# Two engines' queues in written order: TensorE and SyncE in the attention loop of a one-core decoder

## The chip, the cores and the metric

The kernel runs on one core of a Trainium2 chip. A core has TensorE (PE: matrix products, with PEld for the loading of its weights), VectorE (DVE), ScalarE (ACT), GpSimd (POOL) and SyncE (SP, which here only issues DMA transfers). Each engine works through its own list of instructions and waits on semaphores for the others. PSUM is the memory that TensorE writes and VectorE and ScalarE read; it has eight banks. The metric is the device time of the whole program in microseconds (us), as the median of the runs.

## The reference: what is computed

One decoder layer on x of 16 sequences x 128 positions x 256 channels, in float32:

- `x = layernorm(x + attn(x))`, where attn is a gated delta rule with 16 key heads and 32 value heads of 128 channels;
- `x = layernorm(x + xattn(x, ctx))`, a cross attention;
- `x = layernorm(x + ffn(x))`, a mixture of seven experts (two for each token) and one shared expert.

The change touches the first part alone. There the input is projected to q, k and v (`x @ w_qkv`), convolved over four positions in each channel, and put through SiLU; `beta = sigmoid(x @ w_b)` and the decay `g = -exp(A_log) * softplus(x @ w_a + dt_bias)` come from two small projections. The recurrence over positions is

```
S = S * exp(g_t)
delta = (v_t - k_t S) * beta_t
S = S + k_t^T delta
o_t = q_t S
```

and the output is `o * silu(x @ w_z)`, normalised by its root mean square, times `norm_w`, times `w_out`.

## The kernel before

**Units and slots.** The sequences form four groups of four (`G`, `NG`). A unit is one group and one key head with its two value heads, so there are 64 units (`NU`). The recurrence isn't run position by position: for each unit, products of keys and queries with their decays (`pk`, then `lp`) give a lower triangular system, whose diagonal blocks of 32 x 32 are inverted for four units at a time (class `Group`: `begin` transposes the blocks (`Tp`) and forms the factors `bp`, `nbp`; `step` runs on GpSimd, and for the first group of four half of it on VectorE; `turn` transposes the result to `Tt`). The solve itself goes in four block rows: `pt` (multiply by the inverse blocks, `solve`) and `pu` (subtract what earlier rows give, `substitute`).

**The pipeline.** The attention is one loop over slots, `for s in range(NU + DELAY + 3)` (line 548), 74 turns. In slot s the loop works on different units at different stages: on `a` = unit s (projection of k and q, `pjkq`; scan of the decays, `decay`; products), on `v` = s - 6 (projection and convolution of v, `pjv`, `yv`, `vT`), on `m` = s - 7 (transposed values `pv`, first block row), on `p` = s - 8 (middle block rows; gate, `pjz`, `zs`), on `q` = s - 9 (last block row, `attend`: `po`, `og`, their squares `sqs`), and on `o` = s - 10 (`rms_end`, `output`: `pp`, added into `acc`). `psq` sums squares for the unit behind and for `o`. In the written order TensorE's list of a slot is: psq, pjkq of k, pjkq of q, pt (first), pp0 and pp1, po0, pjv0, pjz0, pu (second), pjv1, pp2 and pp3, pt (second), po1, pjz1, pk, pv0, then the next slot's pu (first) and pv1.

**Buffers in PSUM.** Five banks, tag `ps`, go round among pt, pu, pp, po, pk and pv; two banks, tag `pj`, among the projections; one, tag `sm`, holds psq. A projection's bank is free once its readers have finished: for k and q an eviction on ScalarE and three taps (`scalar_tensor_tensor`, line 356) on VectorE, for v two evictions on ScalarE and two taps on VectorE, for z one activation on ScalarE.

**Loads.** SyncE issues each unit's weights (`load_kq`, `load_v`, `load_z`, `load_o`) and decays (`load_dec`), two buffers each. The decays come by way of DRAM: `gates` (line 172) computes beta and the decays of a group, and stores the latter to `dec_d`; `gates([0])` stands ahead of the loop, `gates([1, 2, 3])` in slot 4. The rows of `w_out` are scaled by `norm_w` (`scale_wo`, line 160: two loads to `wor`, one activation on ScalarE, two stores to `wo_d`), in written order in slots 5 to 12; `load_o` reads `wo_d`. `load_x` brings the other groups' part of x in slots 1 to 3.

**What sets the order.** The program is recorded in the order in which Python writes it, and a scheduler then orders each engine's list by priorities and by a model of costs, within what data and buffers permit. `tc.manual_schedule(engines={Pool})` (line 547) excludes GpSimd in the attention loop: its list keeps the written order. TensorE, VectorE, ScalarE and SyncE are ordered by the scheduler. In the program that results, TensorE's list in most slots differs little from the written one: pp2 stands ahead of pjv1 everywhere; in one slot of four the second pu and pp2 stand ahead of pjv0 and pjz0; in another ahead of pjz0 alone; there the second pt is cut into pieces with pp3, po1 and pjv1 between. On SyncE the loads of `scale_wo` for the first two pieces, the three `load_x` and first loads of v and z stand at the head of the loop's list.

Of the kernel before, what the change touches and what calls it, by code (L numbers as in the profile page):

```python
# [18 lines left out]
HK, HV = 16, 32  # L19
G = 4  # L20
# [4 lines left out]
U = 4  # L25
NB, BS = 4, 32
DELAY = 7
# [9 lines left out]
def bc(ap, shape):  # L37
    return ap.to_broadcast(shape)
# [3 lines left out]
def decoder_kernel(  # L42
# [7 lines left out]
    nc = tc.nc  # L50
# [34 lines left out]
    def load_x(g):  # L85
        nc.sync.dma_start(out=acc[:, g * G : (g + 1) * G, :], in_=xv[:, g * G : (g + 1) * G, :])
# [28 lines left out]
    with ExitStack() as st:  # L115
# [6 lines left out]
        def bank(shape, name):  # L122
            return ps.tile(shape, F32, tag="ps", name=name)
# [4 lines left out]
        def transposed_x(g):  # L128
            xT = att.tile([P, 2, 512], F32, tag="xT", bufs=2, name=f"xT{g}")
            for kc in range(2):  # L130
                pt = bank([P, G, P], f"pxT{kc}_{g}_{len(xTs)}")
                for b in range(G):
                    pe.transpose(pt[:, b, :], acc[:, g * G + b, kc * P : (kc + 1) * P], ident)
                dst = xT[:, kc, :].rearrange("p (b t) -> p b t", b=G)
                if kc == 0:
                    act.copy(dst, pt)
                else:
                    vec.tensor_copy(dst, pt)
            return xT

        dec_d = dram.tile([HV, B, S], F32, name="dec_d")
# [30 lines left out]
        def gates(gs):  # L172

            n, b0 = len(gs), gs[0] * G

            def flat(tag, i):
                t = sb.tile([P, G, P], F32, tag=tag, bufs=3, name=f"gt{tag}{i}_{b0}")
                return t.rearrange("p b t -> p (b t)")[:, : n * P]

            apre, tabs, decT = flat("u0", 0), flat("u1", 1), flat("u1", 2)  # L180
            a3 = apre.rearrange("p (b h) -> p b h", h=HV)
            t3 = tabs.rearrange("p (b h) -> p b h", h=HV)
            for i, g in enumerate(gs):
                xT = transposed_x(g)
                if g == 0:
                    xTs[0] = xT
                pab = bank([P, G, 64], f"pab{g}")
                for b in range(G):
                    for kc in range(2):
                        pe.matmul(pab[:, b, :], lhsT=xT[:, kc, b * P : (b + 1) * P],  # L190
                                  rhs=wba[:, kc, :], start=(kc == 0), stop=(kc == 1))
                act.activation(beta[:, g * G : (g + 1) * G, :], pab[:, :, 0:32], AF.Sigmoid)
                vec.tensor_tensor(a3[:, i * G : (i + 1) * G, :], pab[:, :, 32:64],
                                  bc(dtb[:, None, :], [P, G, HV]), ALU.add)
            act.activation(tabs, apre, AF.Abs)
            act.activation(tabs, tabs, AF.Exp, scale=-1.0)
            act.activation(tabs, tabs, AF.Ln, bias=1.0)
            vec.scalar_tensor_tensor(out=tabs, in0=apre, scalar=0.0, in1=tabs,
                                     op0=ALU.max, op1=ALU.add)
            vec.tensor_tensor(t3, t3, bc(expa[:, None, :], [P, n * G, HV]), ALU.mult)  # L200
            act.activation(tabs, tabs, AF.Exp)
            pdt = bank([P, n, P], f"pdt{b0}")
            for i in range(n):
                pe.transpose(pdt[:, i, :], tabs[:, i * P : (i + 1) * P], ident)
            d3 = decT.rearrange("p (g t) -> p g t", t=P)
            vec.tensor_copy(d3, pdt)
            vec.memset(d3[:, :, 0:1], 0.0)
            for b in range(G):
                nc.sync.dma_start(
                    out=dec_d[:, b0 : b0 + n * G, :].rearrange("h (g b) t -> b h g t", b=G)[b],  # L210
                    in_=d3[b * HV : (b + 1) * HV, :, :])

        def behind(inst, after):

# [317 lines left out]
        def at(n):  # L532
            return units[n] if 0 <= n < NU else None
# [3 lines left out]
        for k in range(4):  # L537
            pe.transpose(pcw[:, k, :], cwr[:, :, k], ident[:64, :64])
        vec.tensor_copy(cw.rearrange("p c k -> p k c"), pcw)
        gates([0])  # L540
        units[0].load_dec()
        PIECES = 5
        sqs = None
        done = None


        with tc.manual_schedule(engines={mybir.EngineType.Pool}):
            for s in range(NU + DELAY + 3):
                a, v, m = at(s), at(s - DELAY + 1), at(s - DELAY)
                p, q, o = at(s - DELAY - 1), at(s - DELAY - 2), at(s - DELAY - 3)  # L550
# [7 lines left out]
                def piece(i):  # L558
                    if inv is None:
                        return  # L560
                    at_ = ph * PIECES + i
                    if at_ == 0:
                        inv.begin()
                    if k == 0:

                        if at_ == 0:
                            inv.negate(vec)
                            for j in range(1, 31):
                                last = inv.step(j, vec if j <= 15 else pool)
                                if j == 15:  # L570
                                    a.after = last
                            inv.norms()
                            inv.end()
                        return
                    if at_ == 1:
                        inv.negate(pool)
                    n = 3 * PIECES - 3
                    if 1 <= at_ <= n:
                        for j in range(1 + 30 * (at_ - 1) // n, 1 + 30 * at_ // n):
                            inv.step(j, pool)  # L580
                    if at_ == 2 * PIECES - 1:
                        inv.norms()
                    if at_ == n:
                        inv.end()

                if at(s + 1) is not None:
                    at(s + 1).load_kq()
                    at(s + 1).load_dec()
                if 0 < s < NG:
                    load_x(s)  # L590
                if s == U:
                    piece(0)
                    gates([1, 2, 3])
                if a is not None:
                    if U < s <= U + HK // 2:
                        scale_wo(s - U - 1)
                    if a.hk == 0 and a.g > 0:
                        xTs[a.g] = transposed_x(a.g)
                if v is not None:
                    v.load_v()  # L600
                if p is not None:
                    p.load_z()
                if q is not None:
                    q.load_o()
                jobs = [(m, 0, 0), (p, 1, 1), (p, 0, 2), (q, 1, 3)]
                substitute(f"pu{s}_0", jobs[1:])
                if m is not None:
# [67 lines left out]
    def bank2(shape, name):  # L675
# [4 lines left out]
                      in_=ctx_512.rearrange("b s d -> s b d"))  # L680
# [14 lines left out]
    for i, src in enumerate((bup, bgate)):  # L695
        nc.sync.dma_start(out=brw[:, i].rearrange("p e n -> p (e n)"),
                          in_=src.rearrange("e n -> (e n)").partition_broadcast(P))
# [27 lines left out]
    for t in xg:  # L725
        for i in range(0, TILES, 4):
            n = min(4, TILES - i)
            nc.sync.dma_start(out=t[i * P : (i + n) * P, :].rearrange("(t p) d -> p t d", p=P),
                              in_=zero[:, :n, :])
# [310 lines left out]
    for n in range(-LEAD, len(steps) + 3):  # L1040
# [18 lines left out]
        if n - 3 >= 0 and n % 2 == 1:  # L1059
            m = (n - 3) // 2  # L1060
# [238 lines left out]
```

## Time and profile before

| | us |
|---|---|
| median of the runs | 2191.08 |
| the runs | 2190.01, 2191.08, 2192.49 |
| profiled execution, its own time | 2189.38 |
| profiled execution, span | 2186.8 |
| TensorE busy over the span | 2040.9 |
| slots 10 to 63 (222.24 to 1572.10) | 1349.86 |
| slots 64 to 73, to 1750 | 177.9 |

Times in a profile count from the start of the span; what lies around the span (2.6 us here) is in the execution's own time. A row of the timeline gives start, length, engine, line, operation, output and inputs, how many instructions are folded into it, and in brackets for how long the engine had been idle and what released it. A row of the stages gives a stretch, its length and each engine's busy time in it, and at its end the TensorE clock granted (1.00 is full speed), the share of the DMA engines and GB/s. The chain of waits follows the last instruction back to what released it, step by step, and says which engine each piece of the span falls to.

The profile divides into four: a ramp to 222 us in which the first units pass through the pipeline, the first inversion is awaited, and TensorE is often idle; the steady stage; the drain, in which the last units leave the pipeline; and from 1750 us on the cross attention and the experts.

### The profile page before, as it was taken

The page shows a single profiled execution, that of the slowest core. Times are in us where ns is not written, and L with a number is a line of the kernel's source. Part 1 is how long each engine was busy: PE and PEld are TensorE (multiplying, and loading weights), DVE is VectorE, ACT ScalarE, POOL GpSimd, SP SyncE. Part 2 cuts the span into 40 slices and gives each one's busy share as a digit, 9 for nine tenths or more (in the row PEclk, how much of TensorE's full clock was granted, in tenths as well). Part 3 has the DMA queues.
Part 4 walks back from the last instruction along what each step waited for, and adds up shares of the span by engine and source line. Part 5 has one row for each costly group of instructions (what it writes and reads, how often), then busy time and mean ns, then how long its engine had stood idle before and what let it go on. Part 6 is the DMA issues. An engine that isn't in the chain of part 4 may idle for free.

```text
span 2186.8 us, 40366 instructions
## 1 busy us (share of the span) xinstructions
PE 2040.9 (93%) x14688; PEld 1242.5 (57%) x14688; DVE 1740.3 (80%) x3223; ACT 1316.1 (60%) x2696; POOL 1077.0 (49%) x1639
## 2 busy tenths in 40 slices
PE   4559999999999999999999999999989879989997
PEld 2324556566565666665666656656656534448873
DVE  4657889898999989898999989898856667866545
ACT  4536666667666667666676666676656445554431
POOL 0136473838465564739384655648372143352222
PEclk7779999999999999999999999999999979999998
DMA  6412222222222222222221222222011070013321
GB/s 195 137 48 54 59 59 71 61 65 66 59 64 68 64 64 64 62 69 59 68 64 59 71 61 68 64 59 59 30 40 30 23 262 1 1 56 105 110 80 58
DMA packets 140660, 150.72 MB, mean 69 GB/s; under 512 B 14184, under 2 KB 111472, under 8 KB 140464
## 3 DMA queue, kind: packets, MB, share of 16 engines
q1 hardware_dynamic: 133456, 135.37, 21.9%
q0 software_dynamic: 3072, 8.39, 1.2%
q10 hardware_dynamic: 3936, 4.38, 0.6%
q8 instruction: 118, 1.93, 0.4%
q14 instruction: 78, 0.64, 0.1%
HBM read 125.82 MB, written 22.28 MB: 68 GB/s over the span
## 4 chain that ended last, share of the span: by engine, by line
PE 72%; POOL 10%; DVE 8%; ACT 4%; issue 3%; DMA 3%; SPq 0%; ACTq 0%; POOLq 0%; DVEq 0%
PE pp L467 9%; PE pjv L339 8%; PE pjz L339 8%; PE pjkq L339 8%; PE pt L520 6%; PE po L452 5%; PE pu L505 5%; PE pk L399 4%; PE psc L787 3%; POOL Tp L277 2%; POOL tmp L275 2%; PE pv L439 2%; PE psq L482 2%; PE prg L1123 2%; PE pru L1123 2%
## 5 line engine op out<-in xcount | busy, mean ns | idle before, releaser
L524 ACT COPY u<-pt 32x512 f32<-32x512 f32 x512 | 294.4, 575 | 57.1 <-PE pt L520 48.4
L339 PE MATMUL pjkq<-xT,wkq 128*128 128x512 f32 x512 | 246.0, 621 | 55.9 <-issue 47.3
L509 DVE TENSOR_TENSOR u<-u,pu 32x512 f32<-32x512 f32 x384 | 263.6, 687 | 37.9 <-PE pu L505 27.0
L365 POOL TENSOR_TENSOR yv<-yv,y2v 128x508 f32<-128x508 f32 x128 | 161.8, 1264 | 255.2 <-DVE yv L356 231.8
L467 PE MATMUL pp<-wo,og 128*128 128x256 f32 x1024 | 272.1, 395 | 0.0
L277 POOL TENSOR_TENSOR Tp<-Tp,tmp 128x240 f32<-128x240 f32 (+14 forms) x465 | 253.6, 545 | 36.4
L275 POOL TENSOR_TENSOR tmp<-Tp 128x240 f32<-128x240 f32 (+14 forms) x465 | 239.6, 515 | 62.0 <-DVE Tp L277 33.8
L356 DVE SCALAR_TENSOR_TENSOR ykq<-pjkq,cw,ykq 128x504 f32<-128x504 f32 (+2 forms) x384 | 266.2, 725 | 2.8 <-ACT ykq L349 2.3
L356 DVE SCALAR_TENSOR_TENSOR yv<-pjv,cw,yv 128x504 f32<-128x504 f32 (+1 forms) x256 | 188.9, 738 | 98.7 <-ACT y2v L353 91.6
L339 PE MATMUL pjv<-xT,wv 128*128 128x512 f32 x512 | 250.2, 612 | 16.8 <-issue 7.0
L471 DVE SCALAR_TENSOR_TENSOR acc<-pp,rstd,acc 128x256 f32<-128x256 f32 x512 | 231.5, 477 | 42.9 <-POOL rstd L459 37.1
L459 POOL TENSOR_TENSOR rstd<-var,m_half 128x8 f32<-128x8 f32 x64 | 105.4, 1648 | 320.7 <-DVE ss L493 272.3
L339 PE MATMUL pjz<-xT,wz 128*128 128x512 f32 x512 | 243.7, 598 | 5.9 <-issue 5.9
L366 ACT ACTIVATE vT<-yv 128x512 f32<-128x512 f32 x128 | 80.7, 630 | 252.2 <-POOL yv L365 252.2
L467 PEld LDWEIGHTS pp<-wo,og 128*128 128x128 f32 x1024 | 183.5, 190 | 78.5 <-issue 57.2
L339 PEld LDWEIGHTS pjkq<-xT,wkq 128*128 128x128 f32 x512 | 93.1, 194 | 184.1 <-issue 173.9
L402 DVE TENSOR_TENSOR lp<-pk,e 128x512 f32<-128x512 f32 x256 | 159.3, 682 | 39.7 <-PE pk L399 38.6
L520 PE MATMUL pt<-u,Tt 32*32 32x128 f32 x4096 | 176.2, 272 | 1.6 <-ACT u L442 1.0
L520 PEld LDWEIGHTS pt<-u,Tt 32*32 32x32 f32 x4096 | 116.4, 104 | 105.5 <-issue 35.1
L384 DVE TENSOR_TENSOR_SCAN e<-dec,ident 128x512 f32<-128x512 f32 x128 | 158.4, 1278 | 8.2 <-DMA dec<-dec_d 6.5
L452 PE MATMUL po<-lp,u 128*128 128x128 f32 x1024 | 152.2, 285 | 0.0
L442 ACT ACTIVATE u<-pv,nk 128x128 f32<-128x128 f32 x512 | 147.3, 374 | 6.5 <-PE pv L439 5.8
(226 smaller groups left out, 3619.6 us busy)
## 6 DMA issues: line engine op xcount, KB each, us to landing
dec<-dec_d SPq DMA_DIRECT2D x64, 512.0 KB, 5.2
wkq<-in_L_attn_w_qkv_dram SPq DMA_DIRECT2D x128, 128.0 KB, 5.1
wv<-in_L_attn_w_qkv_dram SPq DMA_DIRECT2D x64, 256.0 KB, 2.6
wz<-in_L_attn_w_z_dram SPq DMA_DIRECT2D x64, 256.0 KB, 2.6
wo<-wo_d SPq DMA_DIRECT2D x64, 256.0 KB, 2.7
rx<-xg SPq DMA_DIRECT2D x44, 128.0 KB, 2.1
yg<-ry SPq DMA_DIRECT2D x44, 128.0 KB, 1.7
xg<-zero SPq DMA_DIRECT2D x10, 512.0 KB, 7.8
```

What stands on the lines that cost most here:

```text
L275: eng.tensor_tensor(tv, bc(T[:, j + 1 :, j : j + 1], [P, n, j]), bc(T[:, j : j + 1, 0:j], [P, n, j]), ALU.mult)
L277: return eng.tensor_tensor(T[:, j + 1 :, 0:j], T[:, j + 1 :, 0:j], tv, ALU.add)
L339: pe.matmul(pj.rearrange("p b t -> p (b t)"), lhsT=ws[kc], rhs=xTs[self.g][:, kc, :], start=(kc == 0), stop=(kc == 1))
L356: inst = vec.scalar_tensor_tensor(out=y[:, :, d:], in0=pj[:, :, : P - d], scalar=c[:, k : k + 1], in1=y[:, :, d:], op0=ALU.mult, op1=ALU.add)
L365: pool.tensor_tensor(y[:, :, 1:], y[:, :, 1:], y2[:, :, 1:], ALU.add)
L402: self.made = vec.tensor_tensor(self.lp[:, r, hf * 2 : hf * 2 + 2], pk, bc(self.e[r][:, hf * 2 : hf * 2 + 2, None, :], [P, 2, 2, P]), ALU. ...
L452: pe.matmul(po[:, b, :], lhsT=self.u_[r][:, b, :], rhs=self.lp[:, r, b, 1, :], start=True, stop=True)
L467: pe.matmul(pp[:, r, :], lhsT=self.og[:, r, b, :], rhs=self.wo[:, r, :], start=True, stop=True)
L471: vec.scalar_tensor_tensor(out=a, in0=pp[:, r, :], scalar=self.rstd[:, r, b : b + 1], in1=a, op0=ALU.mult, op1=ALU.add)
L509: vec.tensor_tensor(u.u_[r][blk], u.u_[r][blk], pu[blk], ALU.subtract)
L520: pe.matmul(pt[blk, b, :], lhsT=groups[u.n // U].Tt[blk, 8 * u.u + G * r + b, :], rhs=u.u_[r][blk, b, :], start=True, stop=True)
L524: act.copy(u.u_[r][blk], pt[blk])
```

## The change

- In the attention loop TensorE and SyncE keep the written order, as GpSimd does. VectorE and ScalarE are still ordered by the scheduler.
- The loads of v, z and w_out of a slot are written one slot earlier: behind the next unit's `load_kq` and `load_dec` come `load_v` for unit s - 5, `load_z` for m and `load_o` for p.
- `gates` returns the function that stores the decays. Group 0's are stored at once; those of groups 1 to 3, computed in slot 4, are stored in slot 5 (`U + 1`), behind the loads just named.

```diff
-            for b in range(G):
-                nc.sync.dma_start(
-                    out=dec_d[:, b0 : b0 + n * G, :].rearrange("h (g b) t -> b h g t", b=G)[b],
-                    in_=d3[b * HV : (b + 1) * HV, :, :])
+
+            def store():
+                for b in range(G):
+                    nc.sync.dma_start(
+                        out=dec_d[:, b0 : b0 + n * G, :].rearrange("h (g b) t -> b h g t", b=G)[b],
+                        in_=d3[b * HV : (b + 1) * HV, :, :])
+
+            return store
...
-        gates([0])
+        gates([0])()
         units[0].load_dec()
         PIECES = 5
         sqs = None
+        stores = []
...
-        with tc.manual_schedule(engines={mybir.EngineType.Pool}):
+        with tc.manual_schedule(engines={mybir.EngineType.Pool, mybir.EngineType.PE,
+                                         mybir.EngineType.SP}):
...
                 if at(s + 1) is not None:
                     at(s + 1).load_kq()
                     at(s + 1).load_dec()
+                if at(s - DELAY + 2) is not None:
+                    at(s - DELAY + 2).load_v()
+                if m is not None:
+                    m.load_z()
+                if p is not None:
+                    p.load_o()
+                if s == U + 1:
+                    for store in stores:
+                        store()
                 if 0 < s < NG:
                     load_x(s)
                 if s == U:
                     piece(0)
-                    gates([1, 2, 3])
+                    stores.append(gates([1, 2, 3]))
...
-                if v is not None:
-                    v.load_v()
-                if p is not None:
-                    p.load_z()
-                if q is not None:
-                    q.load_o()
```

## The prediction

> **What bounds the kernel now.** I read the page first (chain of waits, busy shares), then busy time by stage, then the timelines of SyncE, ScalarE, VectorE and TensorE in the stages that the change touches. The page:
>
> ```profile
> PE 2040.9 (93%) x14688; PEld 1242.5 (57%) x14688; DVE 1740.3 (80%) x3223; ACT 1316.1 (60%) x2696; POOL 1077.0 (49%) x1639
> PE 72%; POOL 10%; DVE 8%; ACT 4%; issue 3%; DMA 3%; SPq 0%; ACTq 0%; POOLq 0%; DVEq 0%
> ```
>
> TensorE (PE) is the bound over all, but by stage the picture differs (columns: stretch, its length, busy time of PE, its weight loads, DVE, ACT, POOL, then PE's clock and DMA):
>
> ```profile
> 28.00:74.00 46.00, 21.71 (x77) 11.27 (x76) 30.23 (x48) 20.04 (x34) 2.74 (x9) 0.76 0.65 178
> 155.00:222.24 67.24, 59.48 (x410) 31.99 (x410) 52.69 (x80) 44.44 (x95) 38.05 (x60) 0.95 0.22 56
> 222.24:1572.10 1349.86, 1336.11 (x10391) 816.89 (x10390) 1217.88 (x2048) 924.29 (x1895) 794.36 (x1180) 1.00 0.23 63
> 1572.10:1750.00 177.90, 163.66 (x1401) 101.88 (x1400) 109.33 (x207) 92.18 (x188) 71.65 (x90) 0.98 0.10 30
> ```
>
> The ramp (slots 0 to 9, to 222 us) is bound by latencies; in the steady stage (slots 10 to 63) PE is busy 99%; in the drain it waits again. From 1743.5 us, the last attention matmul, PE's and ACT's lists are the same in both programs: nothing is counted there.
>
> **The ramp.** The timelines of before's SyncE and ScalarE (start, length):
>
> ```profile
> 9.24 1.02 SPq L166 DMA_DIRECT2D wor<-in_L_attn_w_out_dram  x2
> 25.83 0.88 SPq L166 DMA_DIRECT2D wor<-in_L_attn_w_out_dram  x2
> 28.29 1.74 SPq L209 DMA_DIRECT2D dec_d<-gtu  x4
> 31.25 0.88 SPq L316 DMA_DIRECT2D dec<-dec_d  x2
> ...
> 16.38 1.15 ACT L168 ACTIVATE wor<-wor,normw 128x1024 f32<-128x1024 f32 x1 [6.68 <-DMA wor<-in_L_attn_w_out_dram]
> ```
>
> The scheduler had put the first w_out scalings ahead of everything: ACT idles 6.68 us for them before the gates' sigmoid, and the decays are stored at 28.29 only. In written order they stand in slots 5 to 12. Following ACT's five table loads and activations from where pab is ready, the store goes out at about 23.4 (−4.8; bounds 0 and −6.7, the whole wait) and the first scan at 31.7 instead of 37.8. The three other x loads, which stood ahead of wkq1, now follow a unit's decays; the groups 1 to 3 are wanted in slot 4, past 75 us, so that is free. Their decays' stores move to slot 5, behind wv0: first read in slot 16, hidden by ten slots; if that cover were gone, a late load costs its landing, 5.2 us.
>
> Against this, PE can no longer run a later unit's projections ahead. One ramp slot in strict order: psq 0.43, two projections 4 x 1.02 = 4.1, the second's eviction and three taps 0.69 + 3 x 0.74 = 2.9, SiLU 0.63, pk 3.78, wait for the squares about 0.6: 12.4 us, at half clock. Before, lp1, lp2, lp3 end at 47.1, 62.1 and 76.4; I get 48 (the scans and products of unit 0 end at about 35.5, and a slot follows), 60.9 and 73.5, with some 0.3 of hand-overs in each. So the first inversion (Tp0) starts at 75.5 instead of 80.2; DVE's and POOL's steps are the same, and POOL ends at 119.3 instead of 123.3. Group 1's transposition (Tp1, 179.15) is now followed at once by its small ones: nbp1 comes 4 us after it, not 6, at about 176.5 instead of 185; POOL's inversion paces pv1 of slot 9, 36.5 us later: 213 against 221.7, −8.5. Eight scalings of 1.15 us each now lie in slots 5 to 12: 9.2 us of ACT work, of which I take a third as on the path (ACT is 66% busy there): +3 (bounds 0 and 9.2). **Ramp: −5.5** (bounds −14, if the whole 6.7 of the wait and an 8 us earlier inversion carry through and no scaling costs; and +4, if the scalings cost 9 and the earlier nbp1 gives 5).
>
> The clock in that stage: after 12 us of idle PE runs at half, and with some 4 us of idle it is mixed:
>
> ```profile
> 44.00:56.00 12.00, 0.00 (x0) 0.00 (x0) 8.82 (x14) 4.94 (x10) 1.83 (x6) 0.50 0.73 212
> ...
> 56.21 2.04 PE L339 MATMUL pjkq<-xT,wkq 128*128 128x512 f32 x2 [17.22 <-issue]
> 68.91 1.67 PE L339 MATMUL pjkq<-xT,wkq 128*128 128x512 f32 x2 [4.10 <-issue]
> ```
>
> The Trainium skill ("TensorE: Matmul & The Clock Gate", "HAM oscillation — how this bites in real kernels") says that idle gaps beyond some 3.4 us drop the clock, over and over. It speaks against this change, whose in-order PE idles 4 to 5 us in each ramp slot; the second row agrees only in part (1.67 us, between 1.0 and 2.04). By the rule all three ramp slots stay slow, as I took them; by that row their 4.1 + 3.8 us of matmuls would take 0.82 of it, 1.4 less each, and the sum be lower by 4.
>
> **The steady stage.** Before's list is already near the written one. Four slots, from psq to psq, repeat: 24.06, 24.37, 24.92, 26.25 = 99.6 us. The rows of one undisturbed slot add up to 24.0 (psq .78, pjkq 3.64, two pt 2.0, pp 3.66, two po 2.0, pjv 3.59, pjz 3.53, two pu 2.0, pk 1.72, pv 1.12). So the cycle holds 3.6 us above 4 x 24.0 = 96.0, and **the change breaks even if the in-order waits of four slots sum to 3.6**. Those 3.6 are the price of going around DVE. In the fourth slot:
>
> ```profile
> 879.70 1.05 PE L452 MATMUL po<-lp,u 128*128 128x128 f32 x8
> 881.33 1.96 PE L339 MATMUL pjv<-xT,wv 128*128 128x512 f32 x4 [0.57 <-issue]
> 883.21 1.07 PE L505 MATMUL pu<-u,lp 128*32 128x128 f32 x24
> 884.21 1.13 PE L467 MATMUL pp<-wo,og 128*128 128x256 f32 x4
> 885.18 1.88 PE L339 MATMUL pjz<-xT,wz 128*128 128x512 f32 x4
> 887.86 0.40 PE L520 MATMUL pt<-u,Tt 32*32 32x128 f32 x2
> ...
> 878.64 1.97 DVE L246 STREAM_TRANSPOSE Tp<-ldg 128x1024 f32<-128x1024 f32 x1
> 883.42 0.73 DVE L356 SCALAR_TENSOR_TENSOR ykq<-pjkq,cw,ykq 128x500 f32<-128x500 f32 x1
> ```
>
> The inversion's transposition (1.97 us) delays the convolution taps that free the two pj banks; PE ran pu and pp2 meanwhile, and cut pt (a pair cut off takes 0.33 of PE's time, inside the block 0.06). In written order pjv0 and pjz0 stand ahead of pu: pjv0 waits 0.6 as now, pjz0 waits for the tap that ends at 884.15, 1.1 behind pjv0's end: 24.0 + 1.7 + 0.1 = 25.8 (−0.46). In the third slot the transposition Tt (2 us) makes DVE late in the same way; PE, which found pu and pp2 to do, now waits 1.3 for ykq0 before pjv0: 25.5 (+0.6). In the first and second slot written order has pjv1 directly behind pu, and pp2 behind it; pjv1 takes the bank of pjz0, which ACT's zs0 frees (0.60, plus the hand-over, behind pjz0's end), and pu covers 1.0 of it. ACT reaches zs0 late by its squares: a wait of 0.54 in the first (+0.45 net of a cut less), 0.35 in the second (−0.05 net). Behind each of these waits stand pp, pt and po, so DVE's og and subtractions start later too; they have 10% of slack. Sum +0.55 a cycle, 13.5 cycles: **+7** (bounds: −1 a cycle, where the waits are half of what I count, −13; +1.6, where each of the waits costs a quarter of a microsecond more to wake from, +21). I take a value near the middle, since three of the four waits are read from the ends of rows that stand where they stood.
>
> The loads: SyncE's wo load waits in slot s for pp3 (bank of two), and the next slot's kq, dec, v and z loads stand behind it. Each is issued a slot (24 us) before use and lands in 2.6 to 5.2 us: nothing, as long as that distance stays; if it is gone, about 5 us a slot.
>
> The Trainium skill (same page, "Step-by-step: what each phase is for") says that matmuls stay in program order and only weight loads are pulled ahead. By it none of these waits can be filled by the chip, 4.2 us a cycle; the 0.57 us above, with pu ready behind it, agrees.
>
> **The drain.** In slot 66 DVE's written neighbours change: Tt15, which waits for POOL, now stands ahead of pp1's last accumulation and of og, not behind.
>
> ```profile
> 1626.92 0.68 DVE L454 TENSOR_TENSOR og<-po,zs 128x512 f32<-128x512 f32 x1
> 1631.22 1.93 DVE L287 STREAM_TRANSPOSE Tt<-Tp 128x1024 f32<-128x1024 f32 x1 [3.61 <-POOL Tp L283]
> ```
>
> og then comes at 1633, not 1627, and with it ACT's squares, zs0 and pjv1 behind those; of the 6 us about 5 stay, less 0.1 in each of the five other slots: **+4.5** (bounds −2, where POOL is done earlier, and +8).
>
> **Sum.** −5.5 + 7 + 4.5 = +6. The profiled execution lasted 2189.4 (span 2186.8), 1.7 below the median of 2191.1: 2195.4 by the profile, 2197 as a median.
>
> **The rivals.** (1) Faster: the in-order waits are shorter than the work-arounds. DVE orders its taps anew once pu comes later; with waits of 2.4 instead of 4.2 a cycle, 1.2 under break-even, steady gives −16; ramp −8, drain +4: −20, 2171 (2165 to 2186). For it: PE's own cuts are the visible loss of the fourth slot; against: the taps that pjz0 waits for end where the scan, Tp and pjkq put them, and none of these moves. (2) Same: before's list was near the written one (6098 rows of PE against 5998 after), ramp and steady cancel: 2187 to 2195. (3) Much slower: DVE, 90% busy in the steady stage, is pushed by each PE wait and pushes back; 0.35 a slot more, 54 slots, +19 on +6: 2216 and above. For it: 1217.88 of 1349.86; against: DVE still idles 2.5 us a slot ahead of yv. It decides from some 2.4 us of DVE delay a slot on.
>
> **How the numbers follow.** 0.2% (4.4 us) is about what can be told from no change. The forecast 45% (own range 2195 to 2207), faster 30%, same 15%, much slower 10%. Faster is 0.30, same 0.15, slower 0.55. The range runs from 2174, leaving out the lower third of the first rival, to 2215, leaving out most of the third.
>
> **What would show it.** In the profile after: the first decay store at about 23 and Tp0 near 75 us; psq of slot 10 near 217; slots of about 25.8, 24.6, 24.3 and 25.5, with waits of pjz0 and pjv0 for ykq and of pjv1 for zs; pt whole (x32); in slot 66 og behind Tt. Wrong if pjv0, pjz0 and pjv1 start without waits, or if SyncE's loads show up as what PE waits for.

## The result, and the profile after

The changed kernel takes 2239.9 us (median; 2238.6 to 2240.5) against 2190.6 for the kernel before: a ratio of 1.022, 95% interval 1.021 to 1.023. It is 49 us slower. The prediction was 2197, with a range of 2174 to 2215; the sign was the likelier one, the size was not in the range. The profiled execution has a span of 2238.5, 51.7 more than before; where those lie can be counted from the start of one slot's psq on TensorE to that of the next:

| stage | before | after | difference | predicted |
|---|---|---|---|---|
| to psq of slot 11 | 248.3 | 253.4 | +5.1 | −5.5 |
| slots 11 to 63 | 1323.8 | 1364.1 | +40.3 | +7 |
| slot 64 to the last psq | 168.9 | 173.9 | +5.0 | +4.5 |
| from there to the end | 445.8 | 447.1 | +1.3 | 0 |

The page of the changed kernel, busy shares and chain of waits:

```profile
PE 2025.4 (90%) x14688; PEld 1243.3 (56%) x14688; DVE 1740.7 (78%) x3223; ACT 1324.3 (59%) x2696; POOL 1080.1 (48%) x1639
PE 57%; POOL 18%; DVE 11%; ACT 7%; issue 5%; DMA 2%; ACTq 0%; SPq 0%; POOLq 0%; DVEq 0%
```

TensorE does the same instructions in 15.5 us less busy time (2040.9 to 2025.4), and yet its share of the chain falls from 72% to 57%; POOL, DVE, ACT and "issue" take the rest. TensorE's waits in the steady stage, after (total, number, longest, in us):

```profile
PE pjv L343 <- issue: 26.2, 27, 1.5
PE pjv L343 <- ACT zs L435: 16.4, 41, 0.5
PE pjz L343 <- issue: 14.3, 23, 1.0
PE pt L524 <- DVE u L513: 5.3, 6, 1.4
PE pt L524 <- DVE lp L406: 5.2, 3, 1.7
PE pjv L343 <- ACT u L528: 0.6, 1, 0.6
```

and before:

```profile
PE pjv L339 <- issue: 7.0, 13, 0.6
PE pjz L339 <- issue: 5.9, 14, 2.0
```

That is 68.0 us of waits against 12.9, +55.1. Busy time in the same stage (slots 10 to 63, 1349.9 us before and 1389.1 after) falls from 1336.1 to 1320.9, −15.2. The stage's loss (39.2) is the one less the other, but for waits too small for the list. The trade that the prediction weighed is best read off one cycle of four ordinary slots (length, then TensorE's busy time; before, then after):

```profile
799.10:898.70 99.60, 98.78 (x770) 60.35 (x769) 89.62 (x150) 68.34 (x142) 59.04 (x89) 1.00 0.24 64
819.37:920.43 101.06, 96.78 (x770) 59.46 (x769) 89.26 (x150) 68.88 (x142) 59.63 (x89) 1.00 0.22 63
```

The cuts and re-orderings had cost 2.0 us of busy time a cycle, some 26 in 13 cycles; the waits rise from 0.8 to 4.3 a cycle. In the sum of the stage only 15 of the 26 are seen, since TensorE's busy time in three long slots (below) is some 11 us higher than in others.

**An ordinary slot.** TensorE in a slot of the fourth kind (`s % 4` of 0), changed kernel:

```profile
490.09 1.05 PE L456 MATMUL po<-lp,u 128*128 128x128 f32 x8
491.73 1.95 PE L343 MATMUL pjv<-xT,wv 128*128 128x512 f32 x4 [0.58 <-issue]
494.65 1.95 PE L343 MATMUL pjz<-xT,wz 128*128 128x512 f32 x4 [0.97 <-issue]
496.53 1.07 PE L509 MATMUL pu<-u,lp 128*32 128x128 f32 x24
...
490.92 0.71 DVE L360 SCALAR_TENSOR_TENSOR ykq<-pjkq,cw,ykq 128x500 f32<-128x500 f32 x1
493.81 0.74 DVE L360 SCALAR_TENSOR_TENSOR ykq<-pjkq,cw,ykq 128x500 f32<-128x500 f32 x1
```

The profile names no releaser for these two waits ("issue"), but the ends do: the third tap of k ends at 491.63 and pjv0 starts at 491.73, the third of q at 494.55 and pjz0 at 494.65. pjv0 and pjz0 wait 0.58 and 0.97 us for the taps that free their banks, with pu behind them; the prediction had 0.6 and 1.1. Four slots (`s % 4` of 1, 2, 3 and 0) now take 24.5, 25.0, 25.7 and 25.9 = 101.1 us, against 99.6 before and a forecast of 24.6, 24.3, 25.5 and 25.8 = 100.2.

**Three slots that are not ordinary.** Slots 26, 42 and 58 take 31.6, 31.9 and 32.4 us; before, they took 25.3 each. They alone are 20 of the 51.7 us. Slot 26 on VectorE and TensorE:

```profile
638.66 0.59 DVE L111 TENSOR_SCALAR acc<-acc,mva,rsa 128x256 f32<-128x256 f32 x1 [6.31 <-POOL rsa L106]
639.17 2.47 DVE L406 TENSOR_TENSOR lp<-pk,e 128x512 f32<-128x512 f32 x4
...
640.59 0.37 PE L524 MATMUL pt<-u,Tt 32*32 32x128 f32 x2 [1.73 <-DVE lp L406]
642.41 3.35 PE L524 MATMUL pt<-u,Tt 32*32 32x128 f32 x30 [1.44 <-DVE u L513]
645.69 3.22 PE L471 MATMUL pp<-wo,og 128*128 128x256 f32 x8
...
643.12 0.17 PEld L524 LDWEIGHTS pt<-u,Tt 32*32 32x32 f32 x2 [0.54 <-DVE u L513]
643.85 1.46 PEld L524 LDWEIGHTS pt<-u,Tt 32*32 32x32 f32 x26 [0.55 <-DVE u L513]
```

and before, at the end of the same slot instead of its start:

```profile
644.01 2.04 DVE L111 TENSOR_SCALAR acc<-acc,mva,rsa 128x256 f32<-128x256 f32 x4
```

L111 is the layernorm of the group that has just been finished (unit 15, 31 or 47): four multiplications, which need a power that GpSimd computes (rsa). The scheduler, which still orders VectorE, put the first of them ahead of a unit's products lp. VectorE stands for 6.31 us, and with it the products, the subtractions of pu behind them and TensorE. Then pt and pp, which take 1.08 and 1.99 us in other slots, take 3.35 and 3.22. The stages around them (length, busy times, then TensorE's clock) and the two rows of weight loads (PEld) tell why:

```profile
638.60:642.41 3.81, 0.63 (x4) 0.14 (x3) 3.69 (x7) 0.73 (x2) 2.96 (x7) 0.86 0.01 2
642.41:645.69 3.28, 3.10 (x31) 1.66 (x31) 3.22 (x4) 2.66 (x7) 0.00 (x0) 0.50 0.00 0
645.69:650.00 4.31, 4.31 (x18) 3.66 (x18) 4.28 (x9) 2.70 (x5) 2.36 (x3) 0.71 0.00 0
```

After 3.8 us with only 0.6 us of matmuls the granted clock is 0.50. Not all of the 3.35 us of pt is the clock, though: its second and third part wait for VectorE's next two subtractions, the third until 643.85. So slot 26, 6.7 us longer than the other slots of its kind (31.6 against 25.0), can be divided roughly: 4.6 us of waiting for VectorE (1.73, 1.44, and 1.4 inside pt) and some 2 at the lower clock (about 1 in the rest of pt, 1.2 in pp). Before, the four multiplications stood behind the gating of the slot (at 644.01), when rsa had long been there (at 627.4).

**The ramp.** TensorE and ScalarE in slots 6 to 9 of the changed kernel:

```profile
154.29 1.12 PE L443 MATMUL pv<-ident,vT 128*128 128x128 f32 x4 [4.69 <-ACT vT L370]
178.33 1.11 PE L443 MATMUL pv<-ident,vT 128*128 128x128 f32 x4 [5.39 <-ACT vT L370]
211.46 3.57 PE L343 MATMUL pjv<-xT,wv 128*128 128x512 f32 x4 [4.08 <-issue]
...
174.94 1.15 ACT L168 ACTIVATE wor<-wor,normw 128x1024 f32<-128x1024 f32 x1 [1.82 <-DMA wor<-in_L_attn_w_out_dram]
177.64 0.63 ACT L370 ACTIVATE vT<-yv 128x512 f32<-128x512 f32 x1
```

In the first two rows TensorE stands at pv1, and the next slot's psq and pjkq stand behind it. In ScalarE's list the scaling of a piece of w_out and the copies of ldg stand ahead of vT1; in slot 7 the scaling also waits 1.82 us for its load. In the third row, in slot 9, pjv0 waits without a named releaser.

**The drain.** In slot 66 VectorE stands for Tt15, and og behind it, as forecast:

```profile
1676.84 1.90 DVE L291 STREAM_TRANSPOSE Tt<-Tp 128x1024 f32<-128x1024 f32 x1 [4.73 <-POOL Tp L287]
1678.95 0.67 DVE L458 TENSOR_TENSOR og<-po,zs 128x512 f32<-128x512 f32 x1
```

### The profile page after: what moved, and what is told of

Read it like the earlier page. It is cut to its first block, busy times and chain, and to the rows that moved or that the text cites. A ratio compares the mean times of both kernels' runs of the same rounds, so it can differ in the third digit from the quotient of the medians.

```text
span 2238.5 us, 40186 instructions
## 1 busy us (share of the span) xinstructions
PE 2025.4 (90%) x14688; PEld 1243.3 (56%) x14688; DVE 1740.7 (78%) x3223; ACT 1324.3 (59%) x2696; POOL 1080.1 (48%) x1639
## 3 DMA queue, kind: packets, MB, share of 16 engines
q1 hardware_dynamic: 133456, 135.37, 21.3%
## 4 chain that ended last, share of the span: by engine, by line
PE 57%; POOL 18%; DVE 11%; ACT 7%; issue 5%; DMA 2%; ACTq 0%; SPq 0%; POOLq 0%; DVEq 0%
PE pjv L343 7%; PE pp L471 7%; PE pjkq L343 5%; PE pjz L343 5%; POOL tmp L279 5%; POOL Tp L281 5%; PE pt L524 4%; PE po L456 4%; PE pk L403 3%; PE psc L797 3%; PE pu L509 2%; DVE u L513 2%; POOL nk L270 2%; POOL rstd L463 2%; POOL yv L369 2%
## 5 line engine op out<-in xcount | busy, mean ns | idle before, releaser
L343 PE MATMUL pjv<-xT,wv 128*128 128x512 f32 x512 | 255.4, 622 | 62.1 <-issue 33.1
L360 DVE SCALAR_TENSOR_TENSOR ykq<-pjkq,cw,ykq 128x500 f32<-128x500 f32 (+2 forms) x384 | 266.6, 726 | 11.5 <-ACT ykq L353 10.8
L475 DVE SCALAR_TENSOR_TENSOR acc<-pp,rstd,acc 128x256 f32<-128x256 f32 x512 | 238.1, 477 | 46.1 <-POOL rstd L463 32.2
L279 POOL TENSOR_TENSOR tmp<-Tp 128x240 f32<-128x240 f32 (+14 forms) x465 | 244.5, 526 | 60.4 <-DVE Tp L281 32.2
L471 PE MATMUL pp<-wo,og 128*128 128x256 f32 x1024 | 253.9, 392 | 0.0
L471 PEld LDWEIGHTS pp<-wo,og 128*128 128x128 f32 x1024 | 192.7, 193 | 64.7 <-issue 42.3
L403 PE MATMUL pk<-kq 128*128 128x256 f32 x512 | 132.0, 404 | 46.6 <-ACT kq L365 46.6
L343 PEld LDWEIGHTS pjv<-xT,wv 128*128 128x128 f32 x512 | 88.4, 192 | 147.1 <-issue 104.8
L524 PE MATMUL pt<-u,Tt 32*32 32x128 f32 x4096 | 154.4, 274 | 15.1 <-DVE u L513 9.2
L524 PEld LDWEIGHTS pt<-u,Tt 32*32 32x32 f32 x4096 | 110.5, 105 | 93.9 <-issue 31.5
```

Source lines behind the costliest of these rows:

```text
L279: eng.tensor_tensor(tv, bc(T[:, j + 1 :, j : j + 1], [P, n, j]), bc(T[:, j : j + 1, 0:j], [P, n, j]), ALU.mult)
L343: pe.matmul(pj.rearrange("p b t -> p (b t)"), lhsT=ws[kc], rhs=xTs[self.g][:, kc, :], start=(kc == 0), stop=(kc == 1))
L360: inst = vec.scalar_tensor_tensor(out=y[:, :, d:], in0=pj[:, :, : P - d], scalar=c[:, k : k + 1], in1=y[:, :, d:], op0=ALU.mult, op1=ALU.add)
L403: pe.matmul(pk[:, b].rearrange("p i t -> p (i t)"), lhsT=kq[:, 0, :], rhs=kq.rearrange("p i t -> p (i t)"), start=True, stop=True)
L471: pe.matmul(pp[:, r, :], lhsT=self.og[:, r, b, :], rhs=self.wo[:, r, :], start=True, stop=True)
L475: vec.scalar_tensor_tensor(out=a, in0=pp[:, r, :], scalar=self.rstd[:, r, b : b + 1], in1=a, op0=ALU.mult, op1=ALU.add)
```

## The experiments

Unless said otherwise each is the changed kernel with one edit.

### One engine at a time

SyncE alone in written order (e_sp):

```diff
-        with tc.manual_schedule(engines={mybir.EngineType.Pool, mybir.EngineType.PE,
-                                         mybir.EngineType.SP}):
+        with tc.manual_schedule(engines={mybir.EngineType.Pool, mybir.EngineType.SP}):
```

> The changed kernel with SyncE alone in written order, TensorE ordered by the scheduler as before; loads and stores are written as in the changed kernel. Theory A (the loss comes from TensorE's list, and from what the scheduler makes of VectorE's list around it): slots 10 to 63 take 1350 us as before, the total is 2185 to 2198. Rival B (SyncE's written order delays loads; wv lands in 6.6 us instead of 2.6, wz in 5.5): slots 10 to 63 stay near 1389, the total above 2225.

Measured: 2183.7 us (2182.9 to 2185.2), 0.997 of before, interval 0.995 to 0.998: faster than before by 7 us. Slots 11 to 63 take 1324.4 us (before 1323.8), and slot 11 starts at 240.9 instead of 248.3. Theory A holds.

TensorE alone (e_pe):

```diff
-        with tc.manual_schedule(engines={mybir.EngineType.Pool, mybir.EngineType.PE,
-                                         mybir.EngineType.SP}):
+        with tc.manual_schedule(engines={mybir.EngineType.Pool, mybir.EngineType.PE}):
```

> The changed kernel with TensorE alone in written order, SyncE ordered by the scheduler. Theory A: slots 10 to 63 stay at 1389 us, within 5; the scaling loads may go to the start again, which moves the ramp by some us either way; total 2228 to 2248. Rival B (SyncE): slots 10 to 63 return to 1350, total near 2200.

Measured: 2242.0 (2241.9 to 2242.3), 1.023 of before. Slots 11 to 63 take 1363.5, as in the changed kernel, and the three long slots are there. The two parts of the change have opposite signs: TensorE's order costs some 52 to 56 us, SyncE's with the moved loads gains 7 where TensorE is left to the scheduler; where it is not, 2239.9 against 2242.0 can't be told from no gain.

The loads and stores moved, and both engines left to the scheduler (e_loads; the edit is as above, with Pool alone in the set):

> The kernel before with the loads and the stores moved as in the change, and TensorE and SyncE both ordered by the scheduler. Theory A (the gain of 7 us of SyncE in written order comes from the w_out scalings staying in slots 5 to 12): the scheduler takes those to the start as before, and the total is 2187 to 2195. Rival: the moved loads and stores bring the gain, total 2181 to 2186.

Measured: 2192.2, ratio 1.000 (0.999 to 1.001). The moves alone do nothing.

The kernel before, with SyncE alone in written order and nothing moved (e_sponly):

```diff
-        with tc.manual_schedule(engines={mybir.EngineType.Pool}):
+        with tc.manual_schedule(engines={mybir.EngineType.Pool, mybir.EngineType.SP}):
```

> The kernel before with SyncE alone in written order, and its loads and stores written where they were. Theory A (SyncE runs ahead as far as the two buffers of each weight let it, so a load is issued a slot early wherever it is written; the gain of 7 us is the decay store and the scalings' place): 2181 to 2188. Rival (without the moved loads SyncE in order is late, TensorE waits for wv or wz, or the store of the later groups' decays holds up wkq and dec in slot 4): 2195 or more.

Measured: 2192.9, ratio 1.0006 (0.9995 to 1.0017). That lies between the two: the gain isn't there, though nothing worse than before comes either. So the 7 us need both, the order and the moved loads. By slots, this kernel is 4 us ahead of before at slot 9 and 1 behind at slot 13; slots 10 and 11 take 29.8 and 27.6. Which load or store is late there stays open.

### The three long slots

The layernorm's multiplications tied behind the products of their slot (e_ln):

```diff
-                    ln_apply(*done)
+                    ln_apply(*done, after=a.made if a is not None else None)
```

(`ln_apply` adds an order-only dependency on `after` to each of its four instructions.)

> The changed kernel, with the four layernorm multiplications of a finished group (the first of which stood in VectorE's list ahead of a unit's products, waiting 6.3 us for GpSimd's rsa) tied behind the products of the slot in which they are written. Nothing else moves. Theory A (in each of slots 26, 42 and 58 that wait empties TensorE's queue and drops its clock): these three slots go from 31.6, 31.9 and 32.4 us to about 25.2, so the time falls by 19 to 20 us, to 2220. Rival (these slots are long because a group ends there, with other work of its own): the wait moves to another place, and the time stays within 6 us of 2240.

Measured: 2225.7 (2224.3 to 2227.4), 14.2 us less. Slots 26, 42 and 58 go to 25.7, 25.7 and 25.6, which is 19.0 less. The slots behind them go from 25.7, 25.7 and 26.0 to 26.8, 26.8 and 28.3, where VectorE now does the multiplications ahead of its next work: 4.6 back (in the last, TensorE's clock falls besides; see the end). Theory A holds for the place and the mechanism, and its total missed that the work itself has to go somewhere.

### The ordinary slots

pp2 written ahead of pjv1 (e_pp):

```diff
+                if o is not None:
+                    o.output(2)
                 if v is not None:
                     v.value(1)
                     v.value_end(0)
                 if o is not None:
-                    o.output(2, 3)
+                    o.output(3)
```

> The changed kernel with one line moved: pp2 is written ahead of the second value projection (pjv1) instead of behind it, as the scheduler had it before. Theory A (pjv1 waits for zs0, which frees its bank: 16.4 us in 41 slots of the steady stage, and pp2's 0.9 us covers it): those waits go, the steady stage falls by 14 to 18 us, the total to 2222 to 2226. Rival C (the wait only moves: pt, or the next slot's first projections, wait for VectorE instead): less than 6 us, total above 2234.

Measured: 2209.3 (2209.1 to 2210.8), 30.6 us less, twice the expected. TensorE's waits for zs0 are gone:

```profile
PE pjv L343 <- issue: 32.4, 43, 1.9
PE pjz L343 <- issue: 15.7, 26, 1.0
```

A cycle takes 24.3 + 24.4 + 25.4 + 25.9 = 100.0, 1.1 less, about 14 in 13 cycles. The rest is luck of the scheduler: with this order it puts the four multiplications behind the gating, and slots 26, 42 and 58 take 25.2. That is 20 us less, of which the slots behind them take 3 back. One line moved in TensorE's list thus changed where the layernorm stands in VectorE's.

pu ahead of pjv0 as well, in every slot (e_pu):

```diff
+                jobs = [(m, 1, 0), (m, 0, 1), (p, 1, 2), (p, 0, 3)]
+                substitute(f"pu{s}_1", jobs[1:])
                 if v is not None:
                     v.value(0)
                 if p is not None:
                     p.gate(0)
                 piece(2)
-                jobs = [(m, 1, 0), (m, 0, 1), (p, 1, 2), (p, 0, 3)]
-                substitute(f"pu{s}_1", jobs[1:])
+                if o is not None:
+                    o.output(2)
...
-                    o.output(2, 3)
+                    o.output(3)
```

> The kernel with pp2 ahead of the second value projection, and besides that the second pu written ahead of the first value projection (pjv0) instead of behind the gate's. TensorE and SyncE in written order. Theory A (what is left of TensorE's waits in the steady stage is pjv0 and pjz0 waiting for VectorE's taps, 26.2 and 14.3 us in the changed kernel, and a pu of 1.0 us ahead of them covers most): a cycle of four slots goes from 100.0 to about 97.8 us, the total from 2209 to about 2180. Rival C (pu's three subtractions, 0.7 us each, now stand among the taps, and the waits only move): a gain under 10 us, total above 2199.

Measured: 2206.6 (2205.8 to 2207.3), a gain of 2.7. Rival C holds: the cycle is 100.3, and slots 11 to 63 take 1.6 us more than with pu late. What gain there is lies in the ramp: slot 11 starts at 248.4 instead of 253.6. TensorE waits elsewhere:

```profile
892.47 1.96 PE L343 MATMUL pjz<-xT,wz 128*128 128x512 f32 x4 [0.56 <-PE pjv L343]
895.51 1.99 PE L343 MATMUL pjv<-xT,wv 128*128 128x512 f32 x4 [0.22 <-ACT zs L435]
930.44 0.66 PE L443 MATMUL pv<-ident,vT 128*128 128x128 f32 x4 [0.79 <-ACT vT L370]
```

But the kinds of slot don't move alike: with pu early they take 25.2, 25.2, 25.2 and 24.9 (`s % 4` of 0, 1, 2 and 3), with pu late 25.9, 24.3, 24.4 and 25.4. Early is better only in the two slots that hold an inversion's transposition on VectorE (Tp in the first, Tt in the last); that VectorE's lateness there is the reason is argued, not shown. So pu early in those two alone (e_mix; Tt15 tied too, see below):

```diff
+                early = ph in (0, 3) and s > U + DELAY
+                if early:
+                    substitute(f"pu{s}_1", jobs[1:])
                 if v is not None:
                     v.value(0)
                 if p is not None:
                     p.gate(0)
                 piece(2)
-                substitute(f"pu{s}_1", jobs[1:])
+                if not early:
+                    substitute(f"pu{s}_1", jobs[1:])
```

> TensorE and SyncE in written order, pp2 ahead of pjv1 in all slots, the second pu ahead of pjv0 in the first and last slot of each four (s % 4 of 0 and 3) from slot 12 on, and Tt15 tied behind the gating in slot 66. The two runs before gave 25.89, 24.32, 24.37, 25.40 us for the four kinds of slot with pu late, and 25.17, 25.18, 25.05, 24.86 with pu early. Theory A (each kind of slot keeps its own time): a cycle of 98.7, 17 us less in the steady stage than with pu late, 5.6 less in the drain: 2182 to 2192. Rival C (a slot's late work passes into the next, so the kinds can't be chosen singly): cycle above 99.6, total above 2197.

Measured: 2189.3 (2187.9 to 2194.2), 0.999 of before. Theory A holds: the slots take 25.2, 24.5, 24.4 and 24.9 (same order) = 98.9, less than the 99.6 that the scheduler's list had. So it is not written order as such that loses in the steady stage, but this one.

### The drain

Tt15 tied behind the second gating of slot 66 (e_tt):

```diff
-                    inv.turn(a.made if a is not None else None)
+                    inv.turn(a.made if a is not None else q.gated)
```

> The changed kernel with the last inversion's transposition (Tt15, slot 66) tied behind the second gating of that slot in VectorE's list. Theory A (the prediction's term for the drain: VectorE waits for GpSimd ahead of og): slot 66 goes from 30.2 to about 25 us, the total to 2234 to 2236. Rival: GpSimd itself is late and slot 67 has to wait all the same, the total stays within 1.5 us of 2240.

Measured: 2234.3 (2233.4 to 2235.1), 5.6 us less; slot 66 takes 23.9 instead of 30.2, slot 71 1.7 more. Theory A holds.

### The ramp

The scalings left out, so that the output lacks the factor norm_w (e_nowor):

```diff
-                nc.sync.dma_start(out=self.wo, in_=wo_d[self.hk])
+                nc.sync.dma_start(out=self.wo, in_=w_out[self.hk * 256 : (self.hk + 1) * 256, :]
+                                  .rearrange("(r p) n -> p r n", p=P))
...
-                    if U < s <= U + HK // 2:
-                        scale_wo(s - U - 1)
```

> The changed kernel without the scaling of w_out by norm_w: load_o reads w_out itself, scale_wo isn't called, so the output lacks the factor norm_w. Theory A (the scalings in slots 5 to 12, each with a wait for its load, hold up ScalarE's evictions that TensorE in order waits for): slot 10 starts 8 to 12 us earlier than 228.4, the total is 2228 to 2232; the prediction's +3 for them was too small. Rival B (the ramp is lost by TensorE's order alone): less than 4 us, total above 2236.

Measured: 2231.7 (2230.9 to 2232.5), 8.2 less; slot 10 starts 6.9 earlier, at 221.5. That lies between the two, nearer to theory A: the scalings cost 7 to 8 us, not the 3 of the prediction.

Each scaling tied behind vT1 of the slot before (e_wtie):

```diff
-            act.activation(wor, wor, AF.Copy, scale=normw)
+            behind(act.activation(wor, wor, AF.Copy, scale=normw), after)
```

> The changed kernel with each scaling of w_out tied behind the last value activation (vT1) of the slot before in ScalarE's list; in slots 6 and 7 it had stood ahead of vT1 and waited 1.8 to 2.3 us for its load, while TensorE stood at pv1, 4.7 and 5.4 us. Theory A (those two waits are the price of the scalings, 6.9 us in the ramp by the run without them): slot 10 starts 4 to 6 us earlier, total 2234 to 2236. Rival (what costs is ScalarE's time, not the place): within 2 us of 2240.

Measured: 2240.8 (2240.7 to 2243.0), no gain. Of the two scalings that the expectation names, only that of slot 7 had waited for its load (1.82); that of slot 6, at 150.90, had not. Slot 6 falls from 21.3 to 19.7, but slot 8 rises from 21.9 to 24.9 and slot 9 from 27.2 to 28.0. The rival holds: ScalarE's list of those slots was re-ordered around the scaling (kq, yv and y2v changed places as well), and the time came back two slots later. The same tie in the mixed kernel (e_mixw):

> The kernel of the run before (mixed place of pu, Tt15 tied) with the scalings tied behind vT1 as well. Theory A: the gains add, 4 to 6 us less than that kernel, 2178 to 2187. Rival: the ramp is bound elsewhere once TensorE's list is mixed, no gain over 1.5 us.

Measured: 2192.2 (2188.3 to 2193.9) beside 2189.3, no gain: the rival again.

TensorE left to the scheduler in slots 0 to 10 only (e_split; the loop runs in two stretches with different sets of engines):

```diff
+        E = mybir.EngineType
+        for slots, engines in ((range(11), {E.Pool, E.SP}),
+                               (range(11, NU + DELAY + 3), {E.Pool, E.PE, E.SP})):
+            with tc.manual_schedule(engines=engines):
+                for s in slots:
```

> The changed kernel, with TensorE ordered by the scheduler in slots 0 to 10 and in written order from slot 11 on; SyncE in written order throughout. Theory A (the ramp's loss is TensorE's order in these slots, and nothing of it carries over): slot 10 starts at 214 instead of 228.4 us, the rest is as in the changed kernel, total 2223 to 2228. Rival (the pipeline must fill anyway, and the first slots in written order take the lost time back): 2234 or more.

Measured: 2228.5 (2227.3 to 2230.4), 11.4 less. Slot 10 starts at 212.6, earlier than theory A had it, and itself takes 2.6 of that back (27.6 instead of 25.0); slot 11 starts at 240.2, 13.2 earlier than in the changed kernel and 8.1 earlier than before. Theory A holds but for half a microsecond at the upper end of its range: TensorE's order in the first eleven slots costs 11 to 12 us. In the kernel with SyncE alone, TensorE fills the stand at pv with the next unit's projections:

```profile
143.29 1.98 PE L343 MATMUL pjkq<-xT,wkq 128*128 128x512 f32 x4
145.11 0.60 PE L443 MATMUL pv<-ident,vT 128*128 128x128 f32 x4
```

### The best of both

The mixed order with the ramp left to the scheduler (e_mixs):

> The kernel with the mixed place of pu and Tt15 tied (2189 us, slot 10 at 231.9), with TensorE ordered by the scheduler in slots 0 to 10. Theory A: the gain adds, 14 to 18 us, total 2171 to 2176, below the kernel with SyncE alone in written order (2183.7). Rival: half of it or less, 2181 or more.

Measured: 2177.5 (2175.5 to 2178.5), 0.994 of before, interval 0.992 to 0.996, and 62 us faster than the changed kernel. It gains 11.8 on the mixed kernel, a little short of theory A's figure. Its stages, to be held against the 1323.8 us that slots 11 to 63 took before:

```profile
0.00:242.59 242.59, 164.08 (x889) 92.84 (x889) 159.73 (x276) 126.87 (x229) 85.17 (x151) 0.82 0.36 96
242.59:1562.61 1320.02, 1286.74 (x10201) 791.29 (x10200) 1202.08 (x2013) 911.69 (x1863) 776.18 (x1153) 1.00 0.24 65
```

Compared with before, it gains 5.7 us to slot 11, 3.8 in the steady stage and half a microsecond behind it, 10.0 of its span.

## Why the prediction was wrong

The direction and, for the ordinary slots, the mechanism of the forecast were right: TensorE in order waits for VectorE's taps and ScalarE's zs0, and those waits cost more than the cuts of pt that they replace. The drain was right in its place: Tt15 ahead of og, 5.6 given back by the tie. Its size (+4.5 forecast, +5.0 measured) is in part luck: slot 66 takes 3.4 more, not 5, and slots 65 and 71, which the forecast didn't count, add 1.4 and 0.9. Three terms of the sum were wrong.

**The steady stage's +7 left out the ends of the groups: 20 us.** The step that failed is "Four slots, from psq to psq, repeat", 13.5 times. Every sixteenth slot has work that the four don't show (before, slots 26, 42 and 58 already took 25.3 us where others of their kind took 24.4): a layernorm on VectorE that waits for GpSimd, and in the changed kernel's VectorE list its first multiplication stands ahead of the products. The list of the changed program was there to be read; I followed Tt15, which is the same fault in the drain, and not L111. The run with the tie shows the mechanism, with 19.0 us in the three slots and 14.2 net. Against the prediction's "DVE's og and subtractions start later too; they have 10% of slack": slack of an average is no cover where TensorE stands at once and its clock falls.

**The cycle was +0.55 a cycle, and measured +1.5.** Three of the four kinds of slot came within 0.2 us. The one that failed is the second, forecast 24.3 and measured 25.0: pjv1 waits 0.53 there instead of 0.35, and pjz0 0.24, which the sum left out although before's list already has it:

```profile
833.43 1.95 PE L339 MATMUL pjz<-xT,wz 128*128 128x512 f32 x4 [0.25 <-issue]
854.17 1.95 PE L343 MATMUL pjz<-xT,wz 128*128 128x512 f32 x4 [0.24 <-issue]
```

Over 13 cycles this is some 12 us more than forecast, near the upper bound that the text gave (+1.6 a cycle). To set the in-order waits against the price of the cuts was the right measure, but the break-even of 3.6 us was too high. It was taken from 4 x 24.0 = 96.0 us of undisturbed work; without the cuts four slots still keep TensorE busy for 96.8, so the change broke even at 2.8. The waits are 4.3 (the forecast's own five add up to 3.9, where it says 4.2), and 4.3 − 2.8 is the 1.5.

**The ramp was −5.5, and measured +5.1.** Its first half held: the first store left at 24.5 (forecast 23.4), Tp0 came at 76.4 (75.5), GpSimd's first inversion ended at 119.9 (119.3), and slot 6 starts 3 us earlier than before. From there on the lead was lost: Tp1 came at 177.7, only 1.5 earlier than before, and nbp1 at 180.9, not 176.5. What failed most is "POOL's inversion paces pv1 of slot 9, 36.5 us later: 213". It came at 227.8, 46.9 us after nbp1, while GpSimd itself stood 5.5 us for yv. The distance of 36.5 us was taken from a list in which TensorE runs the next projections ahead of pv; in order, pv1 holds psq and pjkq behind it. The split run shows this part to be worth 11 to 12 us: with TensorE left to the scheduler there, slot 11 starts 8.1 us earlier than before, so the gains forecast for the ramp are there, scalings included, once TensorE may run ahead. The scalings, +3 in the sum, measure 6.9 in the ramp; why a better place for them gives nothing is argued (other evictions moved too), not shown.

Of the rivals, "faster" was wrong on its own decisive point: waits of a cycle stayed above 3.6. "Same" fails since ramp and steady stage both lost. "Much slower" has the right time for another reason: it needed 0.35 us in every slot, and the extra came from three slots (20 us), the cycles (12) and the ramp (10.6). The rule on idle gaps beyond some 3.4 us (the Trainium skill, "TensorE: Matmul & The Clock Gate", "HAM oscillation — how this bites in real kernels") was weighed for the ramp alone, but the clock fell in the steady stage too. The rows there don't agree with the rule as a threshold for one gap: the longest idle gap ahead of the 0.50 above is 1.73 us, with 1.44 behind it and 0.6 us of matmuls in the 3.8; here the measurement decides.

## What to carry to other kernels

Before fixing one engine's order by hand, look at what the scheduler still does with the others: their lists change too, and one early instruction that waits for a slow engine costs more than many small stalls. Sum a periodic loop over its longest period, rare slots included, and read the new lists of all engines there. Fix the order where the work repeats and leave the filling of the pipeline to the scheduler, and choose the written order by kind of slot: pu early was worth −0.7 and −0.6 us in two kinds of slot and +0.8 to +0.9 in the two others.

## What was not expected of the hardware

TensorE's clock fell to 0.50 in the steady stage after 3.8 us in which 0.6 us of matmuls ran, and pp took 3.22 us instead of 1.99. It also fell after a single gap of 1.89 us, but not after each such gap. In the run with the layernorm tied (e_ln), slots 43 and 59 have the same gap ahead of pjv0:

```profile
1079.20 1.96 PE L347 MATMUL pjv<-xT,wv 128*128 128x512 f32 x4 [1.89 <-issue]
1080.99 1.88 PE L347 MATMUL pjz<-xT,wz 128*128 128x512 f32 x4
...
1486.09 2.45 PE L347 MATMUL pjv<-xT,wv 128*128 128x512 f32 x4 [1.89 <-issue]
1488.33 3.12 PE L347 MATMUL pjz<-xT,wz 128*128 128x512 f32 x4
...
1487.40:1490.80 3.40, 3.40 (x5) 1.29 (x4) 2.12 (x6) 1.89 (x4) 0.00 (x0) 0.50 0.01 2
```

In slot 43 the clock stayed at 1.00; in slot 59 it was 0.50 for some 3.4 us, pjz took 3.12 us instead of 1.88, and the slot is 1.5 us longer (28.3 against 26.8). Why it fell in the one and not in the other stays open.

With SyncE in written order some loads took longer to land (wv 6.6 us in the median instead of 2.6, wz 5.5 instead of 2.6; wv 6.1 in the run with SyncE alone, where wz kept 2.7), and wkq less (3.7 instead of 5.1). The steady stage of the run with SyncE alone is none the longer for it (1324.4 against 1323.8).
